# A four-layer gated transformer stack on one core: the order of every engine's queue laid out with a detailed timeline in place of the simple model

## The chip, the cores and the metric

The kernel runs on one NeuronCore of a Trainium2 chip. The metric is device time in microseconds (us) from the launch to the end, as the median of several executions. One execution was also recorded by the hardware profiler; the profile's numbers belong to that execution. In the profile's words, PE is the TensorE's matmul side and PEld its weight loads, DVE is VectorE, ACT is ScalarE, POOL is GpSimd and SP is SyncE, which here only issues DMAs.

## What is computed

Four sublayers update a state x of 2 x 2048 rows by 512 columns, all in float32 at the interface. Each works on the layer-normed state and is added back through a tanh gate:

```python
x = x + tanh(g_xattn[0]) * L0_xattn(layernorm(x), ctx, ...)   # cross-attention, 16 heads of 32
x = x + tanh(g_ffn[0])   * L0_ffn(layernorm(x), ...)          # mixture of depths
x = x + tanh(g_xattn[1]) * L1_xattn(layernorm(x), ctx, ...)   # cross-attention, 16 heads of 64
x = x + tanh(g_ffn[1])   * L1_ffn(layernorm(x), ...)          # ternary weights and a convolution
```

The cross-attentions look at a context of 128 rows for each batch entry. The first feed-forward scores all rows with one router vector, takes the 256 best of each batch entry, runs causal self-attention and a gated MLP (inner size 1365) on these and writes them back; all other rows pass through. The second quantizes its rows to 8-bit integers and its weights to -1, 0, 1, multiplies up to 2048 channels, applies a depthwise convolution of width 3 over the sequence and a Silu, quantizes again and multiplies down to 512.

## The kernel before, in words

The 4096 rows are 32 tiles of 128 rows; four tiles make a block of 512 rows, so there are eight blocks, four to a batch entry. The program is written out in full when it is traced (no loops on the chip). Its stages follow one another but are woven together by generators that are advanced a step at a time from within the attention loops.

*Stage 1 and 3, the cross-attentions* (`cross_attention`). A unit is one head of one block: 128 units in each. For each block, `front` norms the rows (DVE L99 to L104, with a reciprocal root on POOL, L90), transposes them on PE (L113) and copies them on ACT (`xnT`, L241). For a unit, PE computes queries (`pq`, L252, copied to `qT` by DVE L260 or ACT L264) and scores (`sc`, L275); DVE takes the row maxima (`nmx`, L119), ACT the four exponentials with their sums (`A`, L122), DVE the reciprocals (`rden`, L130), and POOL multiplies (L131). Two units later PE transposes the probabilities (`tp`, L293) and DVE copies them (`AT`, L294). Four units together give the values (`po`, L301, copied by ACT L309), and after 16 units `back` adds a bias on POOL to the block's residual rows (`x`, L315), projects (`pp`, L319) and adds (DVE L328).

*Stage 2.* Beside stage 1 a router (L803 to L838, `ranks` with `marks` L859 and counts L865, L923, and a gather L945 to L967) ranks the rows of each finished block. Selected attention (L481 to L593) and its feed-forward (L630 to L655) run once for each batch entry. The ternary weights (L703 to L724) are made beside the feed-forwards. The updated rows are added in place in DRAM by POOL's indirect DMA (L672).

*Stage 4 and 5.* Beside stage 3, each finished block is quantized (`xi`, L1130, transposed at L1136), multiplied up (`ph`, L1152), convolved (`u` L1162, `h` L1164 and L1168) and passed through Silu and Abs on ACT (L1193, L1200); h goes to DRAM (L1199). Four blocks' hidden rows are made integers early (`integers`, L1244 to L1258); the others are reloaded (`x<-h_d`, L1348) and made integers late (L1357 to L1363). Stage 5 multiplies them down (`po`, L1381), adds to the reloaded rows (L1313, L1384) and stores the result (L1385).

*What sets the order of the work.* Each of the five engines runs its own instruction queue from front to back. The kernel doesn't write these queues itself. It calls operations in a program order, on tiles from pools (`bufs` buffers to a tag), and the `TileContext` records them. When the context closes, a scheduler lays out the queues. It runs a simulated machine forward; whenever a queue of that machine can take another instruction, the scheduler gives it the one that is earliest in program order among those whose inputs are ready and whose output has a free buffer. So an instruction that isn't ready in the simulated machine is overtaken by a later one that is. The result is a fixed order for every queue, the buffer of every tile, and the semaphore waits that make this order safe. Table loads of ACT are put in behind this, where an activation function needs another table. On the chip nothing is overtaken any more.

The simulated machine of the kernel before is the library's default, with one duration for each instruction and simple queues. The context is opened with

```python
    with tile.TileContext(nc) as tc:
        flamingo_kernel(tc, aps, out)
```

at line 1505, and this is the only place in the kernel that has to do with the simulated machine.

## Time and profile before

| | us |
|---|---|
| three executions | 1811.35, 1811.64, 1813.81 |
| their median | 1811.64 |
| the profiled execution's own time | 1814.7 |
| its span, first to last instruction | 1813.0 |
| granted TensorE clock in it, mean share of full speed | 0.959 |

Four rough stretches can be told apart in the span: the first cross-attention with the router (0 to about 600 us), the two selected attentions' rest and feed-forwards (600 to 800), the second cross-attention with stage 4 (800 to 1600), and the end, with stage 5 (1600 to 1813).

How to read the rows: a group or a line of the order of time gives start and length, engine, source line, operation, what it writes from what it reads by tile names, the shapes, and in brackets how long the engine was idle before and which work ended that. A wait row gives the waiting work, what it waited for, the total in us, how many times, and the longest.

### The profile page before, as it was taken

To read this page: it belongs to the slowest core of one execution; us is meant where nothing else is said; L and a number is where in the kernel's file an instruction comes from. 1 tells how busy PE (TensorE), PEld (TensorE's weight loads), DVE (VectorE), ACT (ScalarE), POOL (GpSimd) and SP (SyncE) were. 2 spreads that over 40 slices of the span, in tenths; PEclk is the share of its full clock that TensorE was granted. 3 is DMA by queue.
4 is the path that set the end of the run, shared out by engine and by line. 5 is a ranking of instruction groups with operands and counts; after the bars stand their busy time and mean duration, and the time that the engine had idled before them with its cause. 6 is when DMAs were issued, how large, how long until landed. Compare 5 with 4: busy or idle time off the path is not lost.

```text
span 1813.0 us, 25255 instructions
## 1 busy us (share of the span) xinstructions
PE 1662.9 (92%) x8076; PEld 879.3 (49%) x8122; DVE 1296.7 (72%) x2639; ACT 1052.9 (58%) x3074; POOL 525.7 (29%) x669
## 2 busy tenths in 40 slices
PE   6998988899998998989999999999999999888969
PEld 3544444445545665645444444545444454434423
DVE  5777888976766443335357889799798879777956
ACT  1755455345453224425357778788787878754566
POOL 4534434442320021042233243333224332221100
PEclk9999999999999999989999999999999999998989
DMA  6012011121007771730011233334242233246465
GB/s 213 7 65 71 21 63 59 34 89 53 24 36 244 240 233 36 211 86 24 12 59 64 88 114 137 108 114 157 79 148 79 85 114 120 86 187 232 147 223 187
DMA packets 120052, 196.99 MB, mean 109 GB/s; under 512 B 13124, under 2 KB 50756, under 8 KB 116208
## 3 DMA queue, kind: packets, MB, share of 16 engines
q1 hardware_dynamic: 119024, 193.28, 31.2%
q0 software_dynamic: 896, 2.10, 0.5%
q8 instruction: 64, 1.05, 0.2%
q14 instruction: 68, 0.56, 0.1%
HBM read 120.89 MB, written 74.45 MB: 108 GB/s over the span
## 4 chain that ended last, share of the span: by engine, by line
PE 52%; DVE 23%; ACT 8%; DMA 7%; issue 4%; POOL 4%; SPq 0%; POOLq 0%; DVEq 0%; ACTq 0%
PE pp L319 13%; PE pq L252 10%; PE sc L275 4%; PE po L301 4%; PE tp L293 4%; PE ph L1152 3%; ACT A L122 3%; DVE h L1168 3%; DVE nmx L119 2%; DVE AT L294 2%; DVE marks L859 2%; PE pu L645 2%; PE pw L645 2%; PE acc L630 2%; PE po L1381 2%
## 5 line engine op out<-in xcount | busy, mean ns | idle before, releaser
L122 ACT ACTIVATE A<-sc,nmx 128x128 f32<-128x128 f32 x1024 | 361.9, 380 | 168.5 <-DVE nmx L119 136.8
L131 POOL TENSOR_TENSOR A<-A,rden 128x512 f32<-128x512 f32 x256 | 274.4, 1073 | 461.3 <-DVE rden L130 359.1
L319 PE MATMUL pp<-L_wo,OT 128*128 128x512 f32 x768 | 366.3, 608 | 10.7 <-DVE x L328 5.6
L252 PE MATMUL pq<-xnT,L_wq 128*128 128x512 f32 x768 | 349.8, 603 | 1.0 <-DVE x L328 1.0
L122 ACT ACTIVATION_READ_ACCUMULATOR A<-sc,nmx 128x1 f32 x1024 | 224.9, 220 | 0.0
L252 PEld LDWEIGHTS pq<-xnT,L_wq 128*128 128x128 f32 x768 | 144.4, 193 | 161.2 <-issue 153.3
L119 DVE TENSOR_REDUCE nmx<-sc 128x4 f32<-128x512 f32 x256 | 168.7, 679 | 65.2 <-PE sc L275 64.9
L294 DVE COPY AT<-tp 128x512 f32<-128x512 f32 x256 | 173.4, 679 | 58.6 <-PE tp L293 57.9
L319 PEld LDWEIGHTS pp<-L_wo,OT 128*128 128x128 f32 x768 | 136.9, 194 | 153.3 <-issue 130.4
L293 PE MATMUL tp<-ident,A 128*128 128x128 f32 x1024 | 165.4, 286 | 34.4 <-POOL A L131 20.3
L1168 DVE SCALAR_TENSOR_TENSOR h<-u,cw,h 128x512 f32<-128x512 f32 x256 | 191.6, 783 | 5.3 <-ACT h L1164 4.9
L293 PEld LDWEIGHTS tp<-ident,A 128*128 128x128 f32 x1024 | 119.2, 144 | 103.6 <-POOL A L131 44.8
L275 PEld LDWEIGHTS sc<-L_kT,qT 32*128 32x128 f32 (+1 forms) x2048 | 118.9, 197 | 84.0 <-issue 68.8
L275 PE MATMUL sc<-L_kT,qT 32*128 32x128 f32 (+1 forms) x2048 | 148.5, 301 | 9.0 <-ACT A L122 6.0
L1381 PE MATMUL po<-w2q,hq 128*128 128x512 bf16 x501 | 121.1, 394 | 19.2 <-ACT hq L1361 8.2
L1164 ACT ACTIVATE h<-u,cb,cw 128x512 f32<-128x512 f32 x128 | 99.1, 809 | 61.6 <-DVE u L1162 57.0
L301 PE MATMUL po<-AT,L_v 128*32 128x512 f32 (+1 forms) x512 | 120.4, 662 | 8.3 <-DVE AT L294 7.0
L1152 PE MATMUL ph<-xiT,w1q 128*128 128x512 bf16 x477 | 122.7, 380 | 2.8 <-DVE u L1162 0.6
L1162 DVE TENSOR_TENSOR u<-ph,inv_b 128x512 f32<-128x512 f32 x128 | 85.2, 684 | 30.1 <-PE ph L1152 26.1
L1161 POOL COPY u<-carry 128x2 f32<-128x2 f32 x128 | 49.2, 386 | 195.2 <-DVE h L1168 165.5
L309 ACT COPY OT<-po 128x512 f32<-128x512 f32 x96 | 55.8, 587 | 78.1 <-PE po L301 77.6
L315 POOL TENSOR_TENSOR x<-x,L_bo 128x512 f32<-128x512 f32 x64 | 86.4, 1371 | 30.9 <-DMA x<-x_d 15.6
(234 smaller groups left out, 2269.5 us busy)
## 6 DMA issues: line engine op xcount, KB each, us to landing
h_d<-h SPq DMA_DIRECT2D x28, 1024.0 KB, 4.1
x_d<-x SPq DMA_DIRECT2D x64, 256.0 KB, 3.0
hf<-h_d SPq DMA_DIRECT2D x64, 256.0 KB, 3.4
x<-x_d SPq DMA_DIRECT2D x61, 256.0 KB, 4.6
x<-h_d SPq DMA_DIRECT2D x48, 256.0 KB, 5.5
x<-in_x SPq DMA_DIRECT2D x32, 256.0 KB, 3.0
x_d<-xo SPq DMA_DIRECT2D x32, 256.0 KB, 2.0
xf<-x_d SPq DMA_DIRECT2D x32, 256.0 KB, 3.9
```

The costliest lines, as they stand in the source:

```text
L119: nc.vector.tensor_reduce(nmx, sc, AX.X, ALU.max, negate=True)
L122: nc.scalar.activation(out_tile[:, h, :], sc[:, h, :], AF.Exp, bias=nmx[:, h : h + 1], accum_out=den[:, h : h + 1],)
L131: nc.gpsimd.tensor_tensor(out_tile, out_tile, rden.unsqueeze(2).to_broadcast([P, n, width]), ALU.mult,)
L252: nc.tensor.matmul(pq, W.wq[:, d, ts(e, P)], xnT[:, d, :], start=(d == 0), stop=(d == DC - 1),)
L275: nc.tensor.matmul(sc[h][:, t, :], qT[e % cpg][r, ts(t, P)], W.kT[r, b, e, :], start=True, stop=True,)
L293: nc.tensor.transpose(tp[:, t, :], A[:, t, :], ident)
L294: nc.vector.tensor_copy(AT, tp.rearrange("p t n -> p (t n)"))
L301: nc.tensor.matmul(po[h * dh : (h + 1) * dh, :], W.v[:, b, ts(hd, dh)], AT[c * hpc + h], start=True, stop=True,)
L319: nc.tensor.matmul(pp, OT[e][:, ts(i, P)], W.wo[:, e, :], start=(e == 0), stop=(e == nE - 1),)
L1152: nc.tensor.matmul(ph, w1q[:, d, ts(c, P)], xiT[g][:, d, :], start=(d == 0), stop=(d == DC - 1),)
L1168: nc.vector.scalar_tensor_tensor(z, u[:, ds(k, BLK)], cw[:, c, k : k + 1], z, ALU.mult, ALU.add)
L1381: nc.tensor.matmul(po, rows(c), w2q[:, c, :], start=(c == 0), stop=(c == HC - 1))
```

## The change

The context is told to schedule against another simulated machine:

```diff
-    with tile.TileContext(nc) as tc:
+    with tile.TileContext(nc, schedule_with_timeline_sim=True) as tc:
         flamingo_kernel(tc, aps, out)
```

The rule by which the scheduler picks an instruction stays. What changes is the machine that tells it when an engine is free and when an input has arrived: each instruction is there a list of timed events on several devices (sequencer, waiting place, engine, write-back, DMA queues), with a TensorE clock that depends on how busy the array was. So the moments at which instructions become ready differ, and with them who overtakes whom. The operations that the program calls, their operands' shapes and their engines are the same. The order in the queues, the choice of buffer within a tag, and the waits that follow from them may all differ; the placing of table loads follows ACT's new order.

## The prediction

> **What bounds the kernel now.** I read the page's busy times first, then the same split over four stretches of the span, then who ended the TensorE's idle times, and last the order of time around two of the largest.
>
> ```profile
> span 1813.0 us, 25255 instructions
> ...
> PE 1662.9 (92%) x8076; PEld 879.3 (49%) x8122; DVE 1296.7 (72%) x2639; ACT 1052.9 (58%) x3074; POOL 525.7 (29%) x669
> ```
> ```profile
> 0.00:600.00 600.00, 531.74 (x3154) 294.23 (x3155) 454.80 (x1030) 289.50 (x1240) 215.73 (x214) 0.95 0.22 76
> 600.00:800.00 200.00, 184.02 (x809) 121.34 (x808) 76.50 (x183) 61.73 (x142) 28.16 (x30) 0.96 0.54 170
> 800.00:1600.00 800.00, 765.30 (x3377) 384.45 (x3409) 609.45 (x1154) 586.17 (x1534) 258.35 (x372) 0.97 0.27 92
> 1600.00:1813.00 213.00, 181.82 (x740) 79.32 (x753) 155.91 (x274) 115.47 (x159) 23.47 (x54) 0.94 0.59 205
> ```
>
> The first column after the stretch is its length, then busy PE, PEld, DVE, ACT, POOL, granted clock, DMA share, GB/s. The TensorE is the bound in every stretch, and no other engine passes 77% of one. It is idle for 1813.0 - 1662.9 = 150.1 us: 68.3, 16.0, 34.7 and 31.2 us by stretch. An order of the queues removes no work, so it can win from those 150.1 us, and from the clock, which stands at 0.94 to 0.97.
>
> ```profile
> PE tp L293 <- POOL A L131: 20.3, 15, 5.5
> PE pk L184 <- DMA L_wk<-in_L_WkT: 11.2, 1, 11.2
> PE tp L293 <- DVE rden L130: 9.1, 7, 1.9
> PE pt L1136 <- DVE xi L1130: 8.5, 12, 1.7
> PE po L1381 <- ACT hq L1361: 8.2, 4, 6.1
> PE po L1381 <- DVE hq L1363: 8.2, 2, 7.9
> PE po L301 <- DVE AT L294: 7.0, 9, 1.5
> ...
> PE pp L319 <- DVE u L1162: 5.1, 1, 5.1
> ```
>
> These are the longest waits of the matmul queue: total, times, longest. The largest is the attention unit's own chain (scores, maximum, exponentials, division on POOL, transposes). It need not stop the TensorE, since matmuls of other units stand a few places behind. The order of time shows why it does:
>
> ```profile
> 801.49 7.37 POOL L315 TENSOR_TENSOR x<-x,L_bo 128x512 f32<-128x512 f32 x6 [0.26 <-DMA x<-x_d]
> ...
> 808.81 2.05 POOL L131 TENSOR_TENSOR A<-A,rden 128x512 f32<-128x512 f32 x2
> ...
> 809.92 2.11 PE L293 MATMUL tp<-ident,A 128*128 128x128 f32 x8 [5.54 <-POOL A L131]
> ...
> 811.96 0.58 PE L275 MATMUL sc<-L_kT,qT 64*128 64x128 f32 x1
> ```
>
> Six bias additions (L315) for a block's residual, wanted only at its end, stand in POOL's queue ahead of the divisions (L131). The transposes wait 5.5 us, and the next score matmul waits behind them. That is a misplaced order, not a lack of work.
>
> **What the Trainium skill says.** "PSUM — Partial Sum Buffer", section "Engine vs sequencer instructions": the queues of ScalarE, VectorE and GpSimd are strict first in, first out, and matmuls start and complete in program order. The lines above agree (six L315 pass first, for 7.37 us). "TensorE: Matmul & The Clock Gate", Part 1: the array's clock is halved after an idle activity window and released after a busy one. The trace agrees in direction: the 50 us from 800 hold the 5.5 us gap and a granted clock of 0.80; the 50 us after them are fully busy at 1.00. "ScalarE: Activation LUTs", section "What ACT_TABLE_LOAD costs": 1283 ns for a load; the profile has 54 of them at 1283 ns, one pair for nearly each Silu between exponentials.
>
> **The change part by part.** Nothing is removed, and no computing instruction is added. What moves is positions in five queues, with the buffer that a tile gets within its tag, the semaphore waits, and possibly the table loads. The profile of before can't show the new positions, so I price what wrong positions cost now, and take a share of each.
>
> (a) The attention unit's chain, whole program: 20.3 + 9.1 (both above), 2.5 and 0.9 (transposes and values behind the router's count copy L923) and 7.0 make 39.8 us. A schedule that knows POOL's 1073 ns for a division and 1371 ns for a bias addition, with the hand-over between the engines, places transposes later and scores or projections before them. Bounds: nothing to 39.8. I take a third, 13 us, because the chain's length itself (a 679 ns maximum, four 380 ns exponentials, a division, a 679 ns copy) stays, and the four score buffers of the first attention, three in the second, limit how far scores run ahead.
>
> (b) Stage 4 and 5 beside and after the second attention: 8.5 + 8.2 + 8.2 + 5.1 + 2.1 (hidden integers still landing) = 32.1 us. Here real latencies stand behind the waits. The longest, at 1760 us, is a reload:
>
> ```profile
> 1758.52 1.43 DVE L1357 TENSOR_TENSOR x<-x,s_b 128x512 f32<-128x512 f32 x2 [8.34 <-DMA x<-h_d]
> ...
> 1760.35 1.89 PE L1381 MATMUL po<-w2q,hq 128*128 128x512 bf16 x4 [7.85 <-DVE hq L1363]
> ```
>
> SP issues the reload only when a buffer is free. Bounds: a loss of 25 (the rival below) to a gain of 32. I take a fifth, 6 us.
>
> (c) Router, selection, feed-forward and the remaining block seams, each a single wait: 5.4 (L949), 5.6 (L319), 4.9 (L558), 3.7 (L437), 3.3 (L630), 3.2 (L708), 3.0 (L865), 6.0 and 3.0 (L275) = 38.1 us. Bounds: nothing to 38. A fifth, 8 us: many of these chains are serial (a gather needs its rank, a mean needs all its sums). What is left of the 150.1, 28.9 us, lies in smaller rows and in gaps too short for the view; I leave it as it is.
>
> (d) The start: 11.2 us until the first weights land. No order of queues shortens it: 0.
>
> (e) New waits. A new order meets head-of-queue waits of its own; the model can't know jitter of landings or table loads that are placed later. Bounds 0 to 60 (double of what (a) to (c) give back now). I take 8.
>
> (f) The clock. 1 - 0.959 of 1813 us is 74 us of full-clock time not granted. If idle falls by 19 of 150 us, I take 3 us, below the proportional 19/150 x 74 = 9, since many idle bits are shorter than what lowers the clock. Bounds 0 to 9.
>
> (g) SP: its 631 issues move too; all but the tail's reloads have slack, since SP is mostly waiting for data to store (L810 for the projection, 185.4 us in all). 0. ACT's table loads: at most one pair for each Silu, 25 pairs now against 28 Silus before the last block's four, so at most 3 x 2 x 1.28 = 8 us more, on an engine that is 73% busy; 0.
>
> Sum: 13 + 6 + 8 - 8 + 3 = 22 us off the profiled execution's own 1814.7 us (span 1813.0 and 1.7 around it): 1792.7. The median of the runs shown, 1811.64, lies 3.1 below that execution, so 1789.6, rounded to 1790 us. From no change I tell apart about 0.2%, 4 us.
>
> **The rivals.** *The order hardly matters.* In the 700 us from 850 to 1550 the TensorE is busy for 679.14 us, 97%, already, and in both schedules the program's order decides between instructions that are ready. The gain in (a) and the loss in (e) then cancel: 1812. Against it: 110 us of waits with a cause other than data landing.
>
> *Slower, by the tail.* The last 213 us run at 205 GB/s, and their chain of waits passes through transfers:
>
> ```profile
> 1616.79 11.85 DMA h_d<-h
> ...
> 1647.13 15.55 DMA hq<-hq_d
> ...
> 1745.62 12.88 DMA x<-h_d
> ```
>
> If the new order puts reloads behind stores that wait on SP, or lets early integers (L1251 to L1258) be taken late, two more such waits of 12 us each enter the chain, nothing else being left there to hide them: +24, and 1836. It decides once a reload issue slips by more than the six tiles of lookahead (a 687 ns multiplication each, so some 4 us). For it: this stretch is the most fragile. Against it: DMA is busy for only 0.59 of it.
>
> *A large gain.* Half of (a) to (c), 55 us, and a clock at 0.965 instead of 0.959 (0.6% of 1663 = 10): 1812 - 65 = 1747. For it: the waits do have ready matmuls behind them, as at 811.96; against: serial chains in (b) and (c).
>
> **How the numbers follow.** My forecast 0.50 (own range 1772 to 1804), large gain 0.10, no difference 0.12, slower 0.28. So faster by over 0.2%: 0.50 + 0.10 = 0.60; within: 0.12; slower: 0.28. Leaving out half of the large gain and half of the slower case's share gives 1760 to 1836.
>
> **What would show it.** Right: the page's PE busy share rises from 92% towards 93%, the row tp <- POOL A falls from 20.3 to under 14 us, single L315 stand between L131 in POOL's order around the second attention's start, and the granted clock is at or above 0.959. Step (b) is wrong if the last stretch, from the last attention's end, is longer than before; (e) is wrong if the list of PE waits has new rows above 5 us; (g) if ACT holds more than 60 table loads. The whole is wrong if PE's idle time grows, or if it falls and the span does not.

## The result, and the profile after

The kernel after takes 1914.9 us (median of four executions, 1910.6 to 1917.3) against 1811.5 us before in the same comparison: 1.0572 times as long, 95% interval 1.0548 to 1.0597. The prediction was 1790 us, with a range of 1760 to 1836. It was wrong in sign and in size.

The profiled execution of the kernel after has a span of 1912.7 us, 99.7 more than before, at a granted clock of 0.955. Its page begins:

```profile
span 1912.7 us, 25373 instructions
...
PE 1749.3 (91%) x8076; PEld 953.4 (50%) x8122; DVE 1297.1 (68%) x2639; ACT 1052.0 (55%) x3072; POOL 539.1 (28%) x669
```

VectorE and ScalarE are as busy as before to within a microsecond. TensorE has the same number of instructions, but is busy for 86.4 us longer (1662.9 before). The forecast had only looked at idle time. Idle time did grow, from 150.1 to 163.4 us, but that is 13 of 100 us.

Which matmuls became longer? The groups of instructions by line, with different shapes kept apart, first of the kernel before, then of the kernel after. After the shape come the count, the time for which at least one of the group was running, and the mean of one in ns. The count is of instructions; the profile shows two for each of the 512 calls that the program makes in either attention:

```profile
L275 PE MATMUL sc<-L_kT,qT 64*128 64x128 f32 x1024 | 93.6, 298 | 4.1 <-ACT A L122 4.1
...
L275 PE MATMUL sc<-L_kT,qT 32*128 32x128 f32 x1024 | 54.9, 303 | 4.9 <-DVE qT L260 3.0 <-ACT A L122 1.9
```
```profile
L275 PE MATMUL sc<-L_kT,qT 64*128 64x128 f32 x1024 | 129.8, 300 | 11.8 <-ACT A L122 10.4 <-ACT qT L264 1.3
L275 PE MATMUL sc<-L_kT,qT 32*128 32x128 f32 x1024 | 117.7, 293 | 4.9 <-DVE nmx L119 3.0 <-ACT A L122 1.9
```

The score matmuls are busy for 247.5 us instead of 148.5, and all other matmuls together for 12.6 us less. One score matmul still takes 300 ns. What changed is how many run at the same time. In `scores` the time tile is the outer loop and the head the inner one, so neighbours in program order use different rows of the array: four heads of 32 rows in the first attention, two of 64 in the second. "TensorE: Matmul & The Clock Gate" in the Trainium skill, Part 3 "Packing small matmuls — row/col tiling", says that matmuls on different row groups of the array run concurrently. The order of time on TensorE, around 120 us, agrees. Before:

```profile
123.08 1.17 PE L275 MATMUL sc<-L_kT,qT 32*128 32x128 f32 x30
124.17 0.66 PE L293 MATMUL tp<-ident,A 128*128 128x128 f32 x4
```

Thirty score matmuls in 1.17 us. After:

```profile
119.96 0.94 PE L275 MATMUL sc<-L_kT,qT 32*128 32x128 f32 x12
120.82 0.66 PE L293 MATMUL tp<-ident,A 128*128 128x128 f32 x4
121.41 0.49 PE L275 MATMUL sc<-L_kT,qT 32*128 32x128 f32 x4
121.83 0.66 PE L113 MATMUL ptr<-ident,xn 128*128 128x128 f32 x4
122.42 0.48 PE L275 MATMUL sc<-L_kT,qT 32*128 32x128 f32 x2
122.83 0.66 PE L293 MATMUL tp<-ident,A 128*128 128x128 f32 x4
123.42 0.71 PE L275 MATMUL sc<-L_kT,qT 32*128 32x128 f32 x6
```

The 24 of them stand in pieces of 2 to 12 between transposes, and take 2.62 us. By the scheduler's rule this is what comes out if, in the simulated machine, the score buffers of a group come free one after the other: TensorE gets the head that is ready, then something else. That it does so is not shown.

Counting through the two traces separates two losses. First, there are more pieces. The score matmuls stand in 144 unbroken pieces before and 281 after, and a short piece holds TensorE for long: four started 0.42 us before the next shape did (121.41 to 121.83), two 0.41 us, thirty 1.09 us. Second, there is less sharing inside the pieces. Of the score matmuls that directly follow another, 1149 start less than 50 ns after it before, and 533 after; most of the others start 90 to 120 ns after it. An estimate from these traces: the first matmuls of the 137 additional pieces take 48 us, and 479 more neighbours that start one after the other, at some 110 ns each, 53 us. Together that is about the 99 us.

The same busy times, cut into stretches at the first and last score matmul of each attention, show where the 100 us lie. The first column after a stretch's bounds is its length, the next the busy time of PE. Before, the two attentions and the end:

```profile
38.30:514.30 476.00, 430.76 (x2736) 234.97 (x2736) 380.33 (x847) 248.64 (x1140) 192.37 (x176) 0.96 0.14 47
...
791.80:1576.30 784.50, 753.13 (x3330) 379.77 (x3360) 597.34 (x1129) 572.60 (x1495) 254.99 (x368) 0.98 0.27 93
1576.30:1813.00 236.70, 202.18 (x820) 87.97 (x834) 171.14 (x305) 130.92 (x200) 30.34 (x66) 0.93 0.55 191
```

After:

```profile
41.40:554.60 513.20, 492.25 (x2703) 287.68 (x2702) 372.83 (x844) 250.74 (x1144) 188.75 (x174) 0.95 0.13 45
...
830.10:1659.90 829.80, 784.15 (x3318) 403.23 (x3348) 598.20 (x1113) 569.40 (x1494) 269.72 (x366) 0.98 0.25 88
1659.90:1912.70 252.80, 200.87 (x825) 90.61 (x839) 177.49 (x318) 132.71 (x200) 32.01 (x67) 0.89 0.51 179
```

The first attention is longer by 37.2 us, the second by 45.3, the end by 16.1. In the first, TensorE is busy for 61.5 us more and idle for 24.3 less. In the end it is busy for no longer, and the whole 16 us is waiting. The waits of TensorE's queue in the kernel after, total, times and longest:

```profile
PE ptr L437 <- DVE hn L431: 18.1, 2, 14.4
PE pm L1223 <- DVE amax L1206: 16.5, 2, 16.3
PE sc L275 <- ACT A L122: 12.4, 8, 5.8
PE po L1381 <- DVE x L1384: 11.5, 4, 4.1
PE tp L293 <- POOL A L131: 11.3, 11, 3.9
```

The wait that the prediction put first, tp for POOL, did fall, from 20.3 to 11.3 us. Four others took its place.

The largest, at the end, can be followed in the order of time. Before, 81 matmuls of the down projection (po, L1381) stand under the last maxima, and TensorE hardly waits for amax:

```profile
1700.55 18.08 PE L1381 MATMUL po<-w2q,hq 128*128 128x512 bf16 x81
1719.45 0.65 PE L1223 MATMUL pm<-ident,amax 128*128 128x128 f32 x4 [0.83 <-DVE amax L1206]
```

After, these matmuls have been spent earlier. In the trace 61 of them start before the last output projection (pp), where it was 1 before, and 252 instead of 165 before the last ph; none is left under the maxima:

```profile
1804.57 1.03 PE L1152 MATMUL ph<-xiT,w1q 128*128 128x512 bf16 x4
1821.86 1.11 PE L1223 MATMUL pm<-ident,amax 128*128 128x128 f32 x4 [16.25 <-DVE amax L1206]
```

So three suspects stand beside each other: the score matmuls' lost sharing of the array, the down projections spent too early, and something in the other queues. The experiments weigh them.

### The profile page after: what moved, and what is told of

Its sections match the earlier page's. It is cut to its first block, busy times and chain, and to the rows that moved or that the text cites. A ratio compares the mean times of both kernels' runs of the same rounds, so it can differ in the third digit from the quotient of the medians.

```text
span 1912.7 us, 25373 instructions
## 1 busy us (share of the span) xinstructions
PE 1749.3 (91%) x8076; PEld 953.4 (50%) x8122; DVE 1297.1 (68%) x2639; ACT 1052.0 (55%) x3072; POOL 539.1 (28%) x669
## 4 chain that ended last, share of the span: by engine, by line
PE 47%; DVE 25%; DMA 11%; ACT 11%; issue 3%; POOL 1%; SPq 1%; DVEq 0%; ACTq 0%; POOLq 0%
PE pq L252 9%; PE pp L319 8%; PE sc L275 6%; DVE h L1168 4%; PE tp L293 4%; DMA h_d<-h 4%; PE po L1381 3%; PE po L301 3%; ACT A L122 2%; DVE nmx L119 2%; DVE AT L294 2%; DVE marks L859 2%; PE ph L1152 2%; ACT h L1193 2%; DVE u L1162 2%
## 5 line engine op out<-in xcount | busy, mean ns | idle before, releaser
L131 POOL TENSOR_TENSOR A<-A,rden 128x512 f32<-128x512 f32 x256 | 279.3, 1098 | 507.0 <-DVE rden L130 382.8
L319 PE MATMUL pp<-L_wo,OT 128*128 128x512 f32 x768 | 361.6, 607 | 2.5 <-DVE qT L260 2.0
L275 PE MATMUL sc<-L_kT,qT 32*128 32x128 f32 (+1 forms) x2048 | 247.5, 296 | 16.8 <-ACT A L122 12.4
L275 PEld LDWEIGHTS sc<-L_kT,qT 32*128 32x128 f32 (+1 forms) x2048 | 194.6, 190 | 125.1 <-issue 85.8
L1168 DVE SCALAR_TENSOR_TENSOR h<-u,cw,h 128x512 f32<-128x512 f32 x256 | 198.8, 797 | 12.3 <-ACT h L1164 11.6
L293 PE MATMUL tp<-ident,A 128*128 128x128 f32 x1024 | 166.6, 290 | 22.2 <-POOL A L131 11.3
L1381 PE MATMUL po<-w2q,hq 128*128 128x512 bf16 x502 | 122.7, 397 | 17.9 <-DVE hq L1363 9.8
L1152 PE MATMUL ph<-xiT,w1q 128*128 128x512 bf16 x476 | 127.3, 381 | 12.7 <-DVE u L1162 6.3
L1163 POOL COPY carry<-u 128x2 f32<-128x2 f32 x128 | 53.1, 416 | 240.0 <-DVE u L1162 232.1
L301 PE MATMUL po<-AT,L_v 128*32 128x512 f32 (+1 forms) x512 | 115.0, 667 | 2.8 <-DVE AT L294 1.4
L1162 DVE TENSOR_TENSOR u<-ph,inv_b 128x512 f32<-128x512 f32 x128 | 86.3, 681 | 24.3 <-PE ph L1152 23.9
L315 POOL TENSOR_TENSOR x<-x,L_bo 128x512 f32<-128x512 f32 x64 | 86.3, 1373 | 40.4 <-DMA x<-x_d 26.4
```

The source lines that it names most:

```text
L131: nc.gpsimd.tensor_tensor(out_tile, out_tile, rden.unsqueeze(2).to_broadcast([P, n, width]), ALU.mult,)
L275: nc.tensor.matmul(sc[h][:, t, :], qT[e % cpg][r, ts(t, P)], W.kT[r, b, e, :], start=True, stop=True,)
L293: nc.tensor.transpose(tp[:, t, :], A[:, t, :], ident)
L301: nc.tensor.matmul(po[h * dh : (h + 1) * dh, :], W.v[:, b, ts(hd, dh)], AT[c * hpc + h], start=True, stop=True,)
L319: nc.tensor.matmul(pp, OT[e][:, ts(i, P)], W.wo[:, e, :], start=(e == 0), stop=(e == nE - 1),)
L1152: nc.tensor.matmul(ph, w1q[:, d, ts(c, P)], xiT[g][:, d, :], start=(d == 0), stop=(d == DC - 1),)
```

## The experiments

Times are medians; a ratio is against the kernel before, measured beside it on the same chip, with its 95% interval. Kernels that were measured on different chips are best compared by their ratios. "Simple" is the kernel before, "timeline" the kernel after. An edge marked NoSync only says which instruction stands first in a queue; it waits for nothing. The scheduler then lays out everything else anew, the buffers and the semaphore waits too. The last five columns are us; like the sums of waits they come from each kernel's own profiled execution, and line numbers are those of the kernel concerned. In the diffs, NoSync and Sync stand for the dependency object that the code passes, and its label is left out.

| kernel | us | ratio | first attention | second | end | score matmuls busy | PE idle |
|---|---|---|---|---|---|---|---|
| simple (before) | 1811.5 | 1 | 476.0 | 784.5 | 236.8 | 148.5 | 150 |
| timeline (after) | 1914.9 | 1.0572 | 513.2 | 829.8 | 252.8 | 247.5 | 163 |
| timeline_pinned | 1879.3 | 1.037 | 494.0 | 813.8 | 249.5 | 196.1 | 182 |
| simple_pinned | 1814.5 | 1.0006 | 480.5 | 780.8 | 235.4 | 139.4 | 153 |
| simple_by_head | 1854.5 | 1.0242 | 502.9 | 806.4 | 237.2 | 224.3 | 125 |
| simple_by_head_s1 | 1830.6 | 1.0089 | 510.2 | 780.2 | 232.8 | 191.6 | 133 |
| timeline_grouped | 1891.9 | 1.0443 | 494.7 | 822.6 | 252.8 | 154.4 | 224 |
| simple_grouped | 1817.6 | 1.001 | 484.3 | 787.3 | 235.8 | 122.7 | 174 |
| timeline_pinned_abs | 1891.2 | 1.0428 | 492.7 | 823.2 | 252.6 | 197.2 | 187 |
| simple_abs | 1821.1 | 1.0039 | 485.7 | 791.8 | 235.7 | 150.9 | 153 |
| timeline_pinned_tail | 1865.5 | 1.0268 | 495.3 | 814.4 | 234.8 | 195.4 | 172 |
| timeline_pe_of_simple | 1909.9 | 1.0523 | 517.5 | 839.9 | 234.5 | 147.0 | 228 |
| timeline_others_of_simple | 2029.7 | 1.1176 | 530.5 | 911.4 | 257.4 | 249.0 | 221 |
| simple_others_of_timeline | 2076.9 | 1.1445 | 561.1 | 934.3 | 257.9 | 226.5 | 277 |
| timeline_as_written | 1949.7 | 1.075 | 532.1 | 851.3 | 242.0 | 138.1 | 270 |
| timeline_as_written_tail | 1949.6 | 1.0722 | 533.2 | 858.5 | 239.5 | 134.3 | 276 |
| simple_as_written | 1872.5 | 1.0299 | 495.7 | 825.9 | 236.9 | 120.3 | 219 |
| timeline_pe_dve_of_simple | 1862.5 | 1.0275 | 480.7 | 818.1 | 244.8 | 150.2 | 181 |
| timeline_pe_act_of_simple | 1914.1 | 1.0561 | 511.4 | 842.2 | 230.5 | 153.0 | 221 |
| timeline_pe_pool_sp_of_simple | 1917.0 | 1.0584 | 510.8 | 846.2 | 239.6 | 150.9 | 225 |

### The score matmuls' order alone

The edit ties each score matmul behind the one before it in program order (timeline_pinned; simple_pinned is the same on the simple model):

```diff
-            for t in range(TB):
-                for h in range(hpc):
...
-                    nc.tensor.matmul(
+            last = None
+            order = [(t, h) for t in range(TB) for h in range(hpc)]
+            for t, h in order:
...
+                m = nc.tensor.matmul(
...
+                if last is not None:
+                    tc.add_manual_dep(m.ins, last.ins.name, NoSync)
+                last = m
```

> The detailed timeline as in the changed kernel, but the score matmuls of one group of heads are tied in program order (one row tile after the other: head 0, 1, 2, 3 for the first 128 rows, then again), by edges that only fix the order in the queue. Theory A (the slowdown is the score matmuls' lost sharing of the array: 841 of their neighbours were on other row tiles before, 411 after, and their busy time rose from 148.5 to 247.5 us): busy time of sc falls to 150 to 180 us and the time to 1810 to 1850 us. Rival B (the new order's waits in the middle and the tail, e.g. 16.3 us before pm, 14.4 us before the transposes of the selected rows, and reloads on the chain of waits): sc may fall, but the time stays at 1885 us or more, since the TensorE then waits instead.

> The simple model as in the kernel before, with the same edges: a control on what the edges do by themselves. Only 39 pairs of neighbours on the same row tile are to be removed. Theory A: sc 140 to 150 us busy, time 1805 to 1820 us. Rival B says the same here; a time above 1830 us would mean that the edges themselves cost, and the run above could not be read.

Measured: 1879.3 us, ratio 1.037 (1.0335 to 1.0406); the control 1.0006 (0.9993 to 1.002). The pin takes 36 of the 103 us back, a third, and leaves the rest. Neither theory's window for the time is met. The score matmuls are still busy for 196 us, since the scheduler goes on putting other matmuls between the pieces of a group: the trace has 280 pieces, as many as without the pin, while 1019 neighbours again start less than 50 ns apart. So the pin tests the sharing inside the pieces, and not their number.

The reverse edit writes the order head by head into the simple model (`order = [(t, h) for h in range(hpc) for t in range(TB)]`), in both attentions, or only in the first:

> The simple model, but with the score matmuls of a group called and tied head by head (four of one row tile, then four of the next), all else in the order of before as far as the scheduler keeps it. Theory A: about 1024 x 107 ns = 110 us for each of the two attentions, so sc 215 to 245 us busy instead of 148.5, and the time rises by 60 to 100 us to 1870 to 1910 us, with no change of the simulated machine. Rival B: the score matmuls fit into gaps, and the time stays below 1840 us.

> As the run before, but head by head only in the first attention, where four heads of 32 rows share the array; the second keeps program order. Theory A: sc of the 32-row form goes from 54.9 to about 110 us busy, and the time rises by 40 to 60 us, to 1850 to 1870 us, so that the four-way sharing carries most of it. Rival B: below 1830 us.

Measured: ratio 1.0242 (1.021 to 1.0274), 44 us, and 1.0089 (1.0061 to 1.0118), 16 us. The score matmuls of simple_by_head:

```profile
L276 PE MATMUL sc<-L_kT,qT 64*128 64x128 f32 x1024 | 119.1, 291 | 2.7 <-ACT A L122 2.7
L276 PE MATMUL sc<-L_kT,qT 32*128 32x128 f32 x1024 | 105.2, 296 | 6.3 <-DVE qT L260 6.3
```

That is 224.3 us, 75.8 more than before, in about as many pieces as before (137 against 144), for 44 us of time: TensorE's idle time fell from 150 to 125 us. The busy time is what Theory A expected; both times lie between the two theories' windows. So the lost sharing costs time by itself, shown from both sides, but a microsecond of it is worth only some 0.6 us: part of it lies where TensorE would have waited.

### Whole groups, waiting for all their buffers

timeline_grouped adds to the pin an edge (this one a real wait) from the exponentials that free the group's last buffer to the group's first matmul, so that a group can run without a break:

```diff
+                if last is None and len(exps) >= gate:
+                    tc.add_manual_dep(m.ins, exps[-gate].ins.name, Sync)
```

> The detailed timeline, the score matmuls tied in program order as in timeline_pinned, and besides the first of a group waits for the exponentials that free all the buffers the group needs, so that a group can run without a break. Theory A2 (the lost sharing costs its whole 99 us of busy time, and pinning brought back only half because the heads' buffers still come free one at a time): sc about 145 to 165 us busy, time 1835 to 1860 us, and what is left over before (30 us or so) is idle time of the second attention and of the tail (13 to 14 and 16 us in the two runs so far). Rival B2 (waiting for all buffers stalls the TensorE by as much as the sharing saves): sc falls, the time stays at 1870 to 1890 us.

> The simple model with the same grouping. Theory A2: the sharing rises a little over that of before (908 neighbours on other row tiles against 841), sc 125 to 145 us busy, and the time is 1790 to 1812 us. Rival B2: the wait for all buffers delays the softmax chain, idle time of the TensorE in the attentions grows by 20 us or more, and the time is 1820 us or more.

Measured: 1.0443 (1.0411 to 1.0476) and 1.001 (0.9996 to 1.0024). The score matmuls are busy for 154.4 us, almost as before, and TensorE is idle for 224. This kernel is slower than the pin alone, and neither theory's window for the time is met by either run. The pieces fell from 280 to 191, and the busy time that is saved comes back as waiting. It isn't the wait of the scores for the exponentials, which fell from 26.2 us with the pin alone to 20.2. The largest rise is at the transposes: 13.6 to 24.1 us for POOL's division and 1.4 to 8.4 for VectorE's reciprocal. So in the timeline's order the pieces aren't only a loss. They also fill waits that other engines cause. What the number of pieces costs by itself stays open.

### Abs behind other work

In the chain of waits that ended last in the kernel after, ScalarE's Abs (L1200), which overwrites h in place, stands at the head of its queue until the store of h has landed:

```profile
1707.47 1.81 ACT h L1193
1709.29 8.62 DMA h_d<-h
1718.00 1.92 ACT h L1200
```

The total of such waits is 61.6 us, against 26.3 before. The edit places Abs behind the second following convolution's activation:

```diff
-                nc.scalar.activation(h, h, AF.Abs)
...
+                    waiting.append((h, k))
...
+                if c == 1 and waiting:
+                    finish(*waiting.pop(), z1)
```

`finish` holds Abs, tied by a NoSync edge behind z1 (that activation), and the maxima that follow it.

> The detailed timeline with the score matmuls pinned, and beside it Abs (L1200 of before) placed behind the second following convolution's ScalarE instruction, for 21 of the 28 groups. Theory C (what is left of the loss after the pin is in good part Abs standing at the head of ScalarE's queue while the h store has not landed): ScalarE's wait for the h store falls from 59.9 us to 25 us or less, the stretch from the first to the last 64-row score (813.8 us pinned) and the stretch after it (249.5) get shorter by 15 to 35 us together, and the time goes from 1879 to 1845 to 1865. Rival D (the remainder is spread over other heads of queues, and Abs waits in time that ScalarE has to spare): the wait falls as well, but the time stays at 1873 or above.

> Control: the same later Abs in the simple model's order. Both theories: ScalarE's wait for the h store falls from 26.3 us to 15 or less; theory C lets the time fall by up to 10 us (1800 to 1812), rival D expects 1808 to 1815.

Measured: 1.0428 (1.0403 to 1.0452) and 1.0039 (1.0024 to 1.0053). Both theories expected the wait to collapse; it only fell from 59.9 to 45.7 us (26.3 to 20.6 in the simple order), and both kernels became slower. Perhaps the longer life of the h buffer, with the maxima later too, costs more than the wait; no run shows it. Theory C gets no support from this, though the edit didn't remove the wait it was aimed at.

### The down projections of the last stretch

timeline_pinned_tail ties the first matmul of every down projection behind the last output projection:

```diff
+            if c == 0:
+                tc.add_manual_dep(m.ins, last_pp[0].ins.name, NoSync)
```

> The detailed timeline with the score matmuls pinned, and the first matmul of every down projection (po, L1381 of before) placed behind the last output projection of the second attention (pp, L319). Theory G (the last stretch is longer because down projections pulled ahead of pp delay the last group, and are missing later while TensorE waits for amax): the stretch after the last score falls from 249.5 us to 232 to 242, TensorE's wait for amax from 18 us to under 5, the time from 1879 to 1862 to 1873. Rival H (the last group is late because of VectorE's and ScalarE's queues, and the down projections fill waits that would stand anyway): the stretch stays at 245 or more, the time at 1875 or more.

Measured: 1865.5 us, 1.0268 (1.0238 to 1.0299), and the end stretch 234.8 us instead of 249.5. Theory G's window for both is met. At the wait for amax, the order of time of this kernel:

```profile
1758.99 9.88 PE L1394 MATMUL po<-w2q,hq 128*128 128x512 bf16 x44
1776.90 1.11 PE L1236 MATMUL pm<-ident,amax 128*128 128x128 f32 x4 [8.04 <-DVE amax L1219]
```

Forty-four down projections stand under the maxima again, and the wait is 8.0 us instead of 18.2 in timeline_pinned. It was expected under 5: that part was only half right. For the end stretch the cause is shown: where po stands against pp costs 14.7 of its 16 us.

### One engine's queue at a time

After this 49 us are left (ratio 1.0268), nearly all in the two attentions. The next edits give one engine's queue exactly the order of the other kernel, by NoSync edges from each instruction to the next, and leave the rest to the scheduler:

```diff
         flamingo_kernel(tc, aps, out)
+        laid_down(nc, tc)
...
+def laid_down(nc, tc):
...
+        for a, b in zip(names, names[1:]):
+            tc.add_manual_dep(traced[b], a, NoSync)
```

> Every TensorE instruction stands in the simple model's order; the orders of VectorE, ScalarE, GpSimd and SyncE are the detailed timeline's own choice beside it. Theory E (TensorE's order carries the loss: the score matmuls' lost sharing and, with it, what the pieces of a head do to the rest): 1805 to 1835 us, the score matmuls busy for 135 to 155 us. Rival F (the lost sharing is worth the 36 us that pinning it gave back, and the remaining 66 us are heads of the other engines' queues): 1850 to 1880 us with the score matmuls as short.

> The opposite split: VectorE, ScalarE, GpSimd and SyncE in exactly the simple model's order, TensorE's order the detailed timeline's choice (in the second attention most score matmuls follow one of the same head). Theory E: 1855 to 1900 us. Rival F: the sharing lost in the second attention alone, 1825 to 1850 us.

> VectorE, ScalarE, GpSimd and SyncE in exactly the order of the kernel after; TensorE's order is the simple model's choice beside them (score matmuls about half in one head's row). Theory E: 1830 to 1865 us. Rival F: 1875 to 1915 us, since all the other queues are those of the kernel after.

Measured: ratios 1.0523 (1.0496 to 1.0549), 1.1176 (1.1121 to 1.1231) and 1.1445 (1.1405 to 1.1484). All three miss both theories' windows. Two kernels are far slower than the two that they are made of. In these runs a queue is good only beside the queues that it was laid out with, and exchanging one doesn't split a loss into shares.

The first is the most telling. TensorE's queue is that of the kernel before, instruction for instruction, and its score matmuls are busy for 147.0 us. Yet the span is 1907.4 us, 5 us off the kernel after. All the sharing is back, and almost none of the time. The 94.4 us by which this span is longer than before stand as 77.7 us more of idle time and 18.2 us more of other matmuls, with 1.5 us less of scores. So the other queues, with the buffers and waits that come with them, can make a loss of this size beside a TensorE queue that can't give way.

### TensorE's attention as it is written

The means of the start times in the trace of the second attention show how far the timeline had moved things: taken over all of its instructions, the query projections (pq) start 23.7 us ahead of the scores before and 18.0 us after, and the value products (po, L301) follow the scores by 39.5 us before and 47.1 after. Theory K held that this taking apart was the rest of the loss, although 6 to 8 us is little: a unit takes some 6 us (784.5 us for 128 of them). The edit ties all of pq, sc, tp, po and pp in the order in which they are written:

```diff
-                    nc.tensor.matmul(
+                    m = nc.tensor.matmul(
...
+                    behind_last(tc, m, L)
```

> The detailed timeline with all of the attention's TensorE instructions (pq, sc, tp, po, pp) held in the order in which they are written; everything else is free. Theory K (the rest of the loss is the attention's software pipeline on TensorE, taken apart: scores early, value products late): first-attention stretch 470 to 485 us, second 780 to 800, time 1825 to 1845 (the tail still costs up to 14). Rival L (the rest is heads of VectorE's, ScalarE's and GpSimd's queues): 1865 us or more, with the score matmuls at 140 to 150 us and TensorE idle instead.

> The same, and the down projections po behind the last pp. Theory K: 1812 to 1832 us, within 1% of the kernel before. Rival L: 1850 us or more.

> Control: the same pin in the simple model's order, which hardly departs from it. Both: 1803 to 1822 us.

Measured: 1.075 (1.0692 to 1.0809), 1.0722 (1.0667 to 1.0778), and 1.0299 (1.0247 to 1.0351) for the control. Theory K fell: holding the projections and products back adds 82 us, by the ratios, to timeline_pinned_tail. The times are in Rival L's windows, and TensorE is idle as it expected (270 us). The control missed too, so the pin itself costs. The written order, kept strictly, costs the simple kernel 3%, although the score matmuls are then at their shortest (120 us). So the kernel before also lives on some overtaking on TensorE.

### Which other queue

With TensorE's queue held as before, one further queue is put back:

> TensorE and VectorE in exactly the order of the kernel before, ScalarE, GpSimd and SyncE as the detailed timeline chooses beside them. Theory M (what is left is the order of VectorE's queue, the busiest after TensorE and the one that the softmax passes three times): 1812 to 1835 us. Rival N (it is ScalarE's: exponentials behind other work, Abs waiting at its head for a store): 1870 us or more. Rival O (GpSimd's or the transfers'): 1890 us or more.

> TensorE and ScalarE in exactly the order of the kernel before, the other three as the detailed timeline chooses. Theory M: 1880 to 1930 us. Rival N: 1812 to 1835. Rival O: 1890 or more.

> TensorE, GpSimd and SyncE in exactly the order of the kernel before, VectorE and ScalarE as the detailed timeline chooses. Theory M and rival N: 1880 to 1930 us. Rival O: 1812 to 1835.

Measured: with VectorE's 1.0275 (1.0239 to 1.0311), with ScalarE's 1.0561 (1.054 to 1.0583), with GpSimd's and SyncE's 1.0584 (1.0547 to 1.062), against 1.0523 with TensorE's alone. VectorE's order is the only one that takes time back: 45 us by the ratios, about half. It didn't reach Theory M's window (nor that of a rival); the other two runs are where Theory M expected them. The first attention is then at 480.7 us, within 5 of before. What is left lies in the second attention (818.1 against 784.5) and the end (244.8 against 236.8).

How VectorE's order makes TensorE wait can be read around 262 us of timeline_pe_of_simple, the order of time on three engines:

```profile
262.14 3.80 DVE L104 TENSOR_SCALAR xn<-x,L_ln_mv,L_ln_rstd 128x512 f32<-128x512 f32 x4
262.37 0.63 PE L293 MATMUL tp<-ident,A 128*128 128x128 f32 x4 [0.88 <-DVE AT L294]
262.75 5.71 POOL L315 TENSOR_TENSOR x<-x,L_bo 128x512 f32<-128x512 f32 x4 [2.43 <-DVE xn L104]
265.86 0.16 DVE L130 RECIPROCAL rden<-den 128x4 f32<-128x4 f32 x1
...
268.42 1.22 POOL L131 TENSOR_TENSOR A<-A,rden 128x512 f32<-128x512 f32 x1
...
269.69 1.12 PE L293 MATMUL tp<-ident,A 128*128 128x128 f32 x4 [6.70 <-POOL A L131]
```

Four normalizations (L104, 3.80 us) stand in VectorE's queue ahead of the 0.16 us reciprocal, and four bias additions (L315), which wait for the first of them, stand in POOL's ahead of the division. The transposes wait 6.70 us, and everything in TensorE's fixed order behind them. In the waits of TensorE's queue this row is 47.7 us in timeline_pe_of_simple, and with VectorE's order put back 19.9:

```profile
PE tp L293 <- POOL A L131: 47.7, 18, 6.7
```
```profile
PE tp L293 <- POOL A L131: 19.9, 16, 3.1
```

In the kernel after the scheduler was free to put other matmuls in front of such transposes, so there the row is 11.3 us. That the delay came out as score matmuls in pieces and as later waits instead is argued, not shown.

For the other half the chain of waits of timeline_pe_dve_of_simple gives a candidate. It holds the longest stop of TensorE in that kernel, 13.9 us before ph at 1665.91:

```profile
1648.93 1.47 ACT h L1193
1650.40 11.61 DMA h_d<-h
...
1662.09 1.92 ACT h L1200
1664.01 0.02 issue
1664.03 1.23 DVE h L1201
1665.26 0.61 DVE u L1162
```

Abs waits for the store again (46.4 us in all, 26.3 before), with ScalarE's and SyncE's order still the timeline's. But ScalarE's order put back without VectorE's gained nothing, and the kernel with TensorE's, VectorE's and ScalarE's queues put back together wasn't run. So what makes this half is not shown.

## Why the prediction was wrong, by its steps

- **The opening.** "An order of the queues removes no work, so it can win from those 150.1 us, and from the clock." This is the step that failed first. An order removes no instruction, but it does set how long TensorE is busy with the same ones. The sum had no term for it. It measured +99.0 us on the score matmuls and -12.6 on all others. The price in time is less than that: 36 us came back by the pin, and the reverse edit cost 44.
- **(a), the attention's chain, 13 us won.** The row that it named fell, 20.3 to 11.3 us. The gain didn't follow. The first attention's idle time fell by 24.3 us while its busy time rose by 61.5. The prediction took waits removed as time won, without asking what the queue does in place of the wait. The signs that the prediction named failed as well, but for this row: PE's busy share fell from 92% to 91%, its idle time grew, and single bias additions were to stand between POOL's divisions. At the second attention's start there are again seven in a row, in the order of time on POOL of the kernel after:

```profile
835.23 8.60 POOL L315 TENSOR_TENSOR x<-x,L_bo 128x512 f32<-128x512 f32 x7 [0.70 <-DMA x<-x_d]
843.78 3.03 POOL L131 TENSOR_TENSOR A<-A,rden 128x512 f32<-128x512 f32 x3
```

- **(b), the tail, 6 us won, and the rival "slower, by the tail".** The stretch became longer by 16.1 us. The rival had the place right and a size of the right order, but its point of decision, reload issues that slip, isn't what the runs show: 14.7 of the 16 us came back by placing down projections behind the last pp, an edit that names no transfer. That rival's 1836 us was also far short, since it had nothing for the attentions.
- **(c), single waits, 8 us won.** The wait of ptr for hn rose from 3.7 to 18.1 us. But the stretch in which it lies, between the two attentions, became 2 us shorter (277.5 to 275.5), with 5 us less of busy time. Roughly nothing, where 8 was forecast.
- **(e), new waits, 8 us lost, bounds 0 to 60.** This is the term that was mis-sized, and with it the bound. New rows came as it had named for a miss (pm 16.5, ptr 18.1, po for x 11.5), and the cause that it gave, heads of queues, is right in kind. With TensorE's queue held as before, its idle time alone grew by 77.7 us; putting VectorE's order back takes 45 us off the time, and about as much stays with the other queues.
- **(f), the clock, 3 us won.** It went from 0.959 to 0.955, the other way, with 13 us more of idle time. That many waits are too short to lower it was not tested.
- **(d) and (g).** The first weights still land at 11.2 us, and there are 52 table loads instead of 54: both at nothing, as forecast. But (g) looked at ScalarE's table loads alone. Its waits for the h store more than doubled.

Of the rivals, none was near. That the order hardly matters was argued against with 110 us of waits without a landing behind them; by the prediction's own lines 2.1 of these wait for a landing and 7.85 stand behind a reload. The loss falls into three parts, of different strength. That the order of the score matmuls inside their pieces costs time is shown (a third of the loss). The down projections of the tail are shown (about 15 us). For the rest, about 49 us, it is shown that other queues than TensorE's can make as much, and that VectorE's order is about half of what they make when TensorE's is fixed. How much of the 49 us they make when TensorE's queue is free, and how the other half divides between ScalarE, GpSimd, SyncE, the buffers and how they meet, stays open. The parts need not add, since every edit lays the free queues out anew. No version tried beats the kernel before; the nearest are within 0.1% of it (simple_pinned, simple_grouped).

## What to carry to other kernels

Busy time of an engine isn't a constant of the program: where small matmuls share the array by rows, their order decides it, so compare the busy time of each shape, not only the waits. A wait that disappears from a queue is won only if what stands in its place had to be done anyway and at the same price. And a set of queues is one object: here a finer model of the engines didn't make a better order by being finer, and exchanging a single queue between two orders can be worse than either.

## What was not expected of the hardware

The gain from sharing rows is large even for matmuls of 128 columns. Busy time over 1024 score matmuls is 54 ns for each in the first attention before (54.9 us) and 115 after (117.7); with whole groups (simple_grouped) 40.0 us make 39 ns, and head by head (simple_by_head) 105.2 us make 103. In the second attention, with two heads to a group, it is 81 ns with whole groups (82.7 us) against 116 head by head (119.1). One matmul alone takes 288 to 303 ns in all of these, so the mean of one, which the profile prints, hides it completely. A short piece is dear as well: two score matmuls kept the next shape off TensorE for 0.41 us, and thirty only for 1.09.
